# A four-layer graph network on one Trainium2 core: another quarter product by seven products, an order of sums, and an exchange of two products

## The chip, the cores and the metric

The kernel runs on one core of one Trainium2 chip. The metric is the device time of one execution in microseconds, and lower is better. TensorE does the matrix products (the profile calls it PE, and its weight loads PEld), VectorE (DVE) the additions and subtractions, ScalarE (ACT) copies out of PSUM, GpSimd (POOL) and SyncE (SP) mainly issue transfers between memory and the chip.

## The reference

Four layers follow one another, on `x` of 8 batches, 2048 nodes and 64 features and on one adjacency matrix `adj` of 2048 x 2048, in fp32. Cut to the first layer, and to the products by `adj` of the others:

```python
# layer 0: weights by node, from an embedding; Chebyshev terms x, A x, 2 A (A x) - x
for _ in range(2, K):                       # K = 3
    As.append(2.0 * (A @ As[-1]) - As[-2])
x_g = jnp.einsum('knm,bmc->bnkc', A_stack, x)
out = jnp.einsum('bnki,nkio->bno', x_g, w) + b
x = _layernorm(x + out, axis=-1)
# layer 1: twice  h = A z;  z = relu(h W_i)           then layernorm(x + z)
# layer 2: x W_self + (A x) W_neighbor + bias         then layernorm(x + ...)
# layer 3: x, A x, 2 A (A x) - x, each twice, by W    then layernorm(x + ...)
```

With the 8 x 64 = 512 columns of `x` side by side, every layer needs one or two products of the 2048 x 2048 matrix by a 2048 x 512 one, seven in all. What concerns this change is the first of them, `A x` of layer 0, and the place where the second, `A (A x)`, begins.

## The kernel before

All products by `adj` are done after Strassen: the matrix is cut into quarters A11, A12, A21, A22, the right side `x` into four quarters too, and seven products of sums of quarters take the place of eight. The sums of adj's quarters are S1 = A21 + A22, S2 = S1 - A11, S4 = A12 - S2 and S3 = A11 - A21. Inside a quarter product the same is done once more with blocks of 512 x 512; the sums of a quarter's blocks are made by `inner` (four VectorE additions, the tile `si` in the profile), those of the quarters by `outer` (the tile `so`).

The first product is different from the later ones, since the sums of `adj` don't exist yet. It runs over four slices of `adj` (`ns` = 0 to 3); each slice has 128 rows out of every 512 and comes in four chunks `ch[0]` to `ch[3]` of 1 MB, by column blocks of 512. While TensorE multiplies a slice, VectorE makes the sums of the slice (`prepare`), and POOL writes them to memory (`comb`), from which the later products fetch them. `prepare` is a generator; `put(q, s)` writes the sums of quarters and makes and writes their inner sums. Its steps are called between the products with `next(parts)`. Every addition in it is held in the program's order on VectorE.

Slice 0 is `plain_slice`: two column chunks by plain matmuls, 512 columns wide, then four quarter products by seven products (`two_level`). The chunk's first two tile rows and the rows of `x` that go with them come in small transfers, so that TensorE can begin early: chunk (0,2) on SP's queue in parts of 1, 1 and 2 tile rows (L162), and `x` on ACT's queue as the first 128 columns of tile row 0, the rest of it, tile row 1, and tile rows 2 and 3 (L167). Before the data is there TensorE runs a few matmuls on zeros (`rise`).

Slices 1 to 3 are `fast_slice`, with six products (bank `ps_n`, 16 matmuls of 256 columns each) and one by seven products (bank `ps_i`, 28 matmuls of 128 columns), in this order: p2 = A12 by x(1,0); q3 = A22 by t4, by seven products; pa = A11 by x(0,0), copied to `p1`; pc = S1 by t1; pb = S2 by t2; pe = S4 by x(1,1); and S3 by t3, onto the bank of pb. `done(blk, ...)` adds a product in PSUM to a sum and writes one quarter of the result `hT`. The sums t1 to t4 of x's quarters lie in `T`; `t1` (a different name in the code) are sums of x's blocks, which slice 0 uses and which lie in the second slot of `xy`.

What is left over between the products is done by the `pump`: it holds generators, and `pump.step()` after each half product takes one step of them. `back(ns, p, hT)` is such a job: four transposes of `hT` into `pt_n` and a copy by ScalarE into the second slot of `xy`, where the right side of the next product is put together. Slice 2's four are held back until after slice 3's q3. `keep_t1` stores `hT` to memory. After slice 3 its pairs 0 and 1 go back through `pump.drain()`, its pairs 2 and 3 by `last_back` behind the next product's first step (`pt_y`). `join_bias(h, c)` adds a bias to a quarter of `x` in place, when no product reads that quarter any more.

The next product (`product`, bank names `mma`, `mmb`, `mmc`) starts with A11 by the upper left quarter of that slot.

Buffers that matter: four for the inner sums (tag `C`), three for S1 to S4 (tag `T`), five of tag `t` for `hT` (and, from slice 0 to 1, one for the weights `w3`), four banks for `ps_n`, and two that `ps_i` and `pt_n` share.

Of the kernel before, what the change touches and what calls it, by code (L numbers as in the profile page):

```python
# [9 lines left out]
F32 = mybir.dt.float32  # L10
AF = mybir.ActivationFunctionType
ALU = mybir.AluOpType
# [4 lines left out]
P = 128  # L17
# [87 lines left out]
def kernel(  # L105
# [47 lines left out]
    def slice_chunk(ns, j, parts=(TG,)):  # L153

        a = ring.tile([P, TG, NG, P], F32, tag="a", name="a")
        m = 0
        for n in parts:
            nc.sync.dma_start(a[:, m : m + n], slices[ns, j][:, m : m + n])
            m += n
        return a  # L160
# [1 line left out]
    chunks = {}  # L162

    AHEAD = (2, 3, 0, 1)
    chunks[0, AHEAD[0]] = slice_chunk(0, AHEAD[0], (1, 1, 2))

    for t, n, cols in ((0, 1, slice(0, 2 * F)), (0, 1, slice(2 * F, BF)), (1, 1, slice(0, BF)), (2, 2, slice(0, BF))):  # L167
        t += AHEAD[0] * TG
        nc.scalar.dma_start(xy[:, 0, t : t + n, cols], x[:, t : t + n, cols])
    for j in AHEAD[1:]:  # L170
# [414 lines left out]
    if True:  # L585
# [48 lines left out]
        def prepare(ns, ch, outers):  # L634

            ch = [c.rearrange("p m i n -> p i m n") for c in ch]

            def add(out, a, b, op=ALU.add):

                tc.keep_in_program_order(nc.vector.tensor_tensor(out, a, b, op))  # L640

            def kept(tag, shape, bufs):
                s = sums.tile([P, *shape, GW], F32, tag=tag, name="s" + ("i" if tag == "C" else "o"), bufs=bufs)
                n = "ab"[: len(shape)]
                return s, s.rearrange(f"p {' '.join(n)} (m n) -> p {' '.join(n)} m n", m=TG)

            def keep(q, s0, src):
                dst = comb[q][s0 : s0 + src.shape[1]].rearrange("s p (n c) -> p s n c", n=TG)
                nc.gpsimd.dma_start(dst[:, :, ns], src)

            def inner(q, q00, q01, q10, q11):
                flat, s = kept("C", (4,), 4)
                add(s[:, 0], q10, q11)
                add(s[:, 1], s[:, 0], q00, ALU.subtract)
                add(s[:, 2], q00, q10, ALU.subtract)
                add(s[:, 3], q01, s[:, 1], ALU.subtract)
                if q is not None:
                    keep(q, 4, flat)
                return flat

            def raw(I, J):
                return [ch[2 * J + b][:, 2 * I + a] for a in range(2) for b in range(2)]

            def outer(a, b, op, tag="T"):

                flat, s = kept(tag, (2, 2), 3 if tag == "T" else 4)
                for c in range(2):
                    add(s[:, :, c], a(c), b(c), op)
                return flat

            def rq(I, J):
                return lambda c: ch[2 * J + c][:, 2 * I : 2 * I + 2]

            def sq(s):
                return lambda c: s[:, :, c].rearrange("p a (m n) -> p a m n", m=TG)

            def put(q, s):
                flat = s.rearrange("p a b c -> p (a b) c")
                keep(q, 0, flat[:, :2])
                keep(q, 3, flat[:, 3:])  # L680
                inner(q, *(flat[:, k].rearrange("p (m n) -> p m n", m=TG) for k in range(4)))


            outers[A22] = inner(A22, *raw(1, 1))
            yield
            inner(A12, *raw(0, 1))
            if ns == 0:

                sums_of_blocks()
                outers[A11] = inner(A11, *raw(0, 0))  # L690
                outers[A21] = inner(None, *raw(1, 0))
            outers[S1] = s1 = outer(rq(1, 0), rq(1, 1), ALU.add)
            outers[S2] = s2 = outer(sq(s1), rq(0, 0), ALU.subtract)
            outers[S4] = s4 = outer(rq(0, 1), sq(s2), ALU.subtract)
            if ns == 0:

                s3 = outer(rq(0, 0), rq(1, 0), ALU.subtract, "C")
            yield
            put(S1, s1)
            yield  # L700
            put(S2, s2)
            if ns:
                inner(A11, *raw(0, 0))
            yield
            if ns:
                outers[S3] = s3 = outer(rq(0, 0), rq(1, 0), ALU.subtract)
                yield
            put(S3, s3)
            if ns == 0:
                yield  # L710
            put(S4, s4)
            yield

        with tc.tile_pool(name="p_n", bufs=4, space=PSUM) as p_n, tc.tile_pool(
# [62 lines left out]
            def bank():  # L777
                return p_n.tile([P, GW], F32, tag="mm", name="ps_n")
# [13 lines left out]
            def by_tiles(v):  # L792

                return v.rearrange("p (a b) c -> p a b c", b=2)
# [10 lines left out]
                [by_tiles(xy[:, 0, j * TG : (j + 1) * TG, ts(2 * c + p, 2 * F)]) for j in range(2) for p in range(2)]  # L805
                for c in range(2)
            ]
            t1 = [[by_tiles(xy[:, 1, c:NT:TG, ts(n, 2 * F)]) for n in range(4)] for c in range(2)]
            b4 = [T[3][:, 2 * j : 2 * j + 2, :, ts(p, 2 * F)] for j in range(2) for p in range(2)]
            t4 = xs.tile([P, 4, TG, 2 * F], F32, tag="t4", name="t4")  # L810
            t4 = [by_tiles(t4[:, n]) for n in range(4)]
# [84 lines left out]
            def fast_slice(ns, ch, held, rest):  # L896
# [5 lines left out]
                def raw(I, J):  # L902
                    return lambda j, m: ch[2 * J + j][:, m, 2 * I : 2 * I + 2]

                def summed(q):
                    return lambda j, m: outers[q][:, :, j, ts(m, P)]

                def x_of(h, c):
                    return lambda k, p: xcol(0, h * NT // 2 + k, 2 * c + p)

                def t_of(n):
                    return lambda k, p: T[n - 1][:, k // 2, k % 2, ts(p, 2 * F)]

                def mul(ps, a, b, start=True, steps=2):

                    for p in range(2):
                        for k in range(NT // 2):
                            nc.tensor.matmul(  # L918
                                ps[:, ts(p, GW // 2)], b(k, p), a(k // TG, k % TG),
                                start=(start and p == k == 0), stop=(k == NT // 2 - 1),  # L920
                                skip_group_check=True,
                            )
                        if p < steps:
                            pump.step()
                    return ps

                hT = {}
# [27 lines left out]
                for job in held:  # L955
                    pump.add(back(*job))
                next(parts)
                pa = mul(bank(), raw(0, 0), x_of(0, 0))
                p1 = sums.tile([P, GW], F32, tag="p1", name="p1")
                nc.scalar.copy(p1, pa)  # L960
                nc.vector.tensor_tensor(q3, q3, p1, ALU.add)
                done(0, p2, p1)
                if ns == TG - 1:
# [9 lines left out]
                pb_ = mul(bank(), summed(S2), t_of(2))  # L973
                u2 = plus("u2", pb_, p1)
                nc.vector.tensor_tensor(u2, pc, u2, ALU.add)
                nc.vector.tensor_tensor(p1, pc, p1, ALU.add)
                next(parts)
                pe = mul(bank(), summed(S4), x_of(1, 1))
                done(1, pe, u2)
                if ns == TG - 1:  # L980
                    join_bias(1, 0)
                mul(pb_, summed(S3), t_of(3), start=False)

                done(2, pb_, q3)
                done(3, pb_, p1)
                return [hT[p] for p in range(NP)]

            last_pairs = []
            for ns in range(TG):
                ch = [chunks.pop((ns, j)) for j in range(NG)]  # L990
                if ns == 0:
                    outers = {}
                    parts = prepare(ns, ch, outers)
                    for _ in range(2):
                        next(parts)
                    first4 = plain_slice(ns, ch, outers)
                    next(first4)
                    sums_of_x(0)
                    sums_of_x(1)
                    next(parts)  # L1000
                    next(first4)
                    sums_of_x(2)
                    sums_of_x(3)
                    sums_t(b4, t4)
                    next(first4)
                    next(parts)
                    hT = next(first4)
                    next(parts)
                    w3 = load_weights()
                    load_chunks(1, *AHEAD)  # L1010
                    pump.add(biases())
                else:
                    hT = fast_slice(ns, ch, held, parts if ns == 1 else ())
                for p in range(NP):
                    keep_t1(ns, p, hT[p])

                held = []
                for p in range(NP):
                    if ns == TG - 2:
                        held.append((ns, p, hT[p]))  # L1020
                    elif ns == TG - 1 and p >= NP // 2:
                        last_pairs.append(hT[p])
                    else:
                        pump.add(back(ns, p, hT[p]))
            join_bias(1, 1)
            pump.drain()

# [238 lines left out]
```

## Time and profile before

| what | us |
|---|---|
| median of 3 runs | 1666.83 |
| lowest and highest | 1666.49, 1666.88 |
| profiled execution | 1666.76 |
| its span, first to last instruction | 1665.0 |
| mean granted clock of TensorE | 0.999 |
| first matmul on data (`plain_slice`) | at 5.92 |
| second tile row's first matmul | at 9.81 |
| slice 1 begins (first matmul of p2) | at 58.96 |
| q3 of slice 1, first matmul | at 68.00 |
| pa of slice 1, first matmul | at 74.80 |
| slice 2 begins | at 111.09 |
| slice 3 begins | at 160.54 |
| first transposes of slice 3's result | at 209.99 |
| next product (`mma`), first matmul | at 211.71 |

The span is one execution under the profiler; the time of that execution is 1.76 us longer than its span, which the work before the first and after the last instruction makes up. Times in the text are from the start of the span. "us, x96" beside a line number means 96 instructions of that line; a matmul of the program appears as two records.

### The profile page before, as it was taken

The numbers are of one execution on the slowest core, as the hardware profiler recorded it, in microseconds if no ns is written. First come the engines' busy times: TensorE is split into PE (matmuls) and PEld (weight loads), VectorE is DVE, ScalarE is ACT, GpSimd is POOL, SyncE is SP. The second block draws the span as 40 slices with busy tenths as digits, with TensorE's granted clock in tenths as the row PEclk, the third lists the DMA queues.
The fourth block names the chain that finished last, engine by engine and source line by source line (L and its number), as shares of the span: only waits on it lengthen the run. The fifth ranks groups of instructions, "written<-read, shape, count | busy, mean of one in ns | idle before, by whom it ended". The sixth has DMA issues, their size and how long they took to land.

```text
span 1665.0 us, 21271 instructions
## 1 busy us (share of the span) xinstructions
PE 1656.7 (100%) x8414; PEld 1060.6 (64%) x8414; DVE 965.9 (58%) x1737; ACT 276.0 (17%) x810; POOL 246.1 (15%) x332
## 2 busy tenths in 40 slices
PE   9999999999999999999999999999999999999998
PEld 5988844444444444444454455599998455579998
DVE  5986895656456456655434365873668344453657
ACT  0200110242142144430010011220001011100001
POOL 1221200254155056550000000000000000000000
PEclk9999999999999999999999999999999999999999
DMA  8998899504503600019877867657888866678884
GB/s 318 340 383 310 316 322 326 200 26 162 205 26 129 250 26 26 26 65 364 290 266 278 304 254 257 229 218 272 291 297 299 306 209 233 230 264 294 316 311 167
DMA packets 81074, 391.56 MB, mean 235 GB/s; under 512 B 8944, under 2 KB 25584, under 8 KB 41040
## 3 DMA queue, kind: packets, MB, share of 16 engines
q1 hardware_dynamic: 68288, 346.78, 58.2%
q0 software_dynamic: 11248, 42.08, 6.7%
q10 hardware_dynamic: 1440, 1.35, 0.3%
q8 instruction: 67, 1.10, 0.3%
q14 instruction: 31, 0.25, 0.0%
HBM read 339.85 MB, written 50.33 MB: 234 GB/s over the span
## 4 chain that ended last, share of the span: by engine, by line
PE 95%; DVE 3%; DMA 1%; issue 0%; SPq 0%; DVEq 0%
PE y L1109 20%; PE mmb L277 17%; PE mma L277 12%; PE mmc L277 12%; PE mmb L270 9%; PE ps_n L918 7%; PE mma L270 6%; PE mmc L270 6%; PE z L1161 3%; PE z L1190 2%; PE ps_i L832 1%; DVE si L640 1%; DMA xy<-in_x 1%; PE pt L1152 1%; DMA bias<-in_b_l 0%; DVE so L640 0%
## 5 line engine op out<-in xcount | busy, mean ns | idle before, releaser
L277 PE MATMUL mmb<-a,t 128*128 128x512 f32 x648 | 292.0, 593 | 0.0
L1119 DVE SCALAR_TENSOR_TENSOR xy<-y,e_sb,xy 128x128 f32<-128x128 f32 x512 | 179.6, 351 | 141.2 <-PE y L1109 125.3
L277 PEld LDWEIGHTS mmb<-a,t 128*128 128x128 f32 x648 | 121.5, 190 | 145.3 <-issue 143.5
L1128 POOL TENSOR_TENSOR s<-s 128x512 f32<-128x512 f32 (+2 forms) x192 | 157.4, 820 | 333.0 <-ACT s L1123 322.8
L1123 ACT ACTIVATE s<-y,e_sb 128x128 f32<-128x128 f32 x512 | 139.3, 383 | 231.5 <-PE y L1109 231.5
L228 DVE TENSOR_TENSOR u<-mmb,p 128x512 f32<-128x512 f32 x84 | 57.9, 689 | 176.5 <-PE mmb L277 121.1
L270 PE MATMUL mmb<-t,a 128*128 128x128 f32 x1344 | 156.9, 275 | 0.0
L270 PEld LDWEIGHTS mmb<-t,a 128*128 128x128 f32 x1344 | 153.5, 192 | 0.0
L1109 PE MATMUL y<-wn,xT 64*128 64x512 f32 x512 | 131.5, 590 | 0.0
L1109 PE MATMUL y<-wn,C 64*128 64x512 f32 x512 | 131.2, 589 | 0.0
L1109 PE MATMUL y<-wn,tT 64*128 64x512 f32 x512 | 131.2, 589 | 0.0
L277 PE MATMUL mma<-a,T 128*128 128x512 f32 x256 | 115.5, 594 | 0.0
L277 PE MATMUL mmc<-a,t 128*128 128x512 f32 x216 | 97.3, 592 | 0.0
L295 ACT COPY p<-mma 128x512 f32<-128x512 f32 x42 | 24.7, 588 | 405.8 <-PE mma L277 248.4
L1109 PEld LDWEIGHTS y<-wn,xT 64*128 64x128 f32 x512 | 49.3, 187 | 61.2 <-issue 60.7
L1109 PEld LDWEIGHTS y<-wn,tT 64*128 64x128 f32 x512 | 49.6, 187 | 60.2 <-issue 60.2
L1109 PEld LDWEIGHTS y<-wn,C 64*128 64x128 f32 x512 | 49.5, 187 | 60.3 <-issue 60.3
L277 PE MATMUL mma<-a,xy 128*128 128x512 f32 x192 | 86.6, 594 | 0.3 <-PE pt_n L465 0.3
L277 PEld LDWEIGHTS mma<-a,T 128*128 128x128 f32 x256 | 47.6, 190 | 56.8 <-issue 56.5
L228 DVE TENSOR_TENSOR C<-mmc,C 128x512 f32<-128x512 f32 x48 | 33.2, 692 | 85.9 <-PE mmc L277 75.1
L277 PEld LDWEIGHTS mmc<-a,t 128*128 128x128 f32 x216 | 40.0, 190 | 45.4 <-issue 45.2
L277 PEld LDWEIGHTS mma<-a,xy 128*128 128x128 f32 x192 | 36.0, 190 | 44.4 <-issue 43.8
(160 smaller groups left out, 2127.5 us busy)
## 6 DMA issues: line engine op xcount, KB each, us to landing
a<-comb SPq DMA_DIRECT2D x240, 1024.0 KB, 4.8
a<-in_blocks SPq DMA_DIRECT2D x54, 1024.0 KB, 4.8
comb<-si POOLq DMA_DIRECT2D x28, 1024.0 KB, 6.2
a<-in_slices SPq DMA_DIRECT2D x15, 1024.0 KB, 9.0
comb<-so POOLq DMA_DIRECT2D x15, 512.0 KB, 9.6
t1T<-hT SPq DMA_DIRECT2D x16, 256.0 KB, 4.6
xT<-in_xT SPq DMA_DIRECT2D x16, 256.0 KB, 3.0
tT<-t1T SPq DMA_DIRECT2D x16, 256.0 KB, 3.1
```

What stands on the lines that cost most here:

```text
L228: nc.vector.tensor_tensor(out, a, b, op)
L270: nc.tensor.matmul(to, a[:, k, m, :], xb[:, m, :], start=(start and opens and m == 0), stop=(m == TG - 1), skip_group_check=True,)
L277: nc.tensor.matmul(ps, xb[:, m, :], a[:, :, m, :], start=(start and m == 0), stop=(m == TG - 1), skip_group_check=True,)
L295: nc.scalar.copy(p1, pa)
L640: tc.keep_in_program_order(nc.vector.tensor_tensor(out, a, b, op))
L918: nc.tensor.matmul(ps[:, ts(p, GW // 2)], b(k, p), a(k // TG, k % TG), start=(start and p == k == 0), stop=(k == NT // 2 - 1), skip_group_ ...
L1109: mm = nc.tensor.matmul(y[:, b, :], terms[n][half, ts(k, P)], wn[half, n, h * DH : (h + 1) * DH, :], start=(n == 0), stop=(n == 2),)
L1119: nc.vector.scalar_tensor_tensor(acc, y[:, :, ts(d, F)], e, acc, ALU.mult, ALU.add)
L1123: nc.scalar.activation(s[:, d], y[:, :, ts(d, F)], AF.Copy, scale=e)
L1128: nc.gpsimd.tensor_tensor(s[:, :n], s[:, :n], s[:, n : 2 * n], ALU.add)
L1161: nc.tensor.matmul(z[:, k, :], aT[:, ts(k, P)], wd[:, w, :], start=(n == 0), stop=(n == len(terms) - 1),)
L1190: nc.tensor.matmul(z[n][:, k], xT[half, ts(k, P)], w[half], start=True, stop=True)
```

## The change

Four things are changed, all within the first product and the step to the second.

1. The first chunk comes in parts of 1 and 3 tile rows instead of 1, 1 and 2, and the rows of `x` beside it as two parts of tile row 0 and one of tile rows 1 to 3.
2. In slice 1, A11's inner sums are made right after A12's, ahead of S1, and A11 by x(0,0) becomes a `two_level` product, with the block sums `t1` that slice 0 has left. For that the two halves of `t1` change places: what belongs to columns 0 now lies where slice 1's own result will be put, and not where slice 0's goes. The product has no pump steps of its own.
3. In slice 0, `put(S3)` comes before `put(S2)`; one call of `next(parts)` at its end falls away, so that `put(S2)` and `put(S4)` are both done in slice 1, after A22's inner sums.
4. In slice 3 the last two products change places: S3 by t3 comes before S4 by x(1,1) and gets a bank of its own, with `q3` plus the S2 product made by an addition of its own. The results of pairs 0 and 1 are then complete before the last product, and their store and their `back` jobs are put in there, two to a half product (`n=2`).

```diff
-    chunks[0, AHEAD[0]] = slice_chunk(0, AHEAD[0], (1, 1, 2))
+    chunks[0, AHEAD[0]] = slice_chunk(0, AHEAD[0], (1, 3))
-    for t, n, cols in ((0, 1, slice(0, 2 * F)), (0, 1, slice(2 * F, BF)), (1, 1, slice(0, BF)), (2, 2, slice(0, BF))):
+    for t, n, cols in ((0, 1, slice(0, 2 * F)), (0, 1, slice(2 * F, BF)), (1, 3, slice(0, BF))):
...
             inner(A12, *raw(0, 1))
+            if ns == 1:
+                outers[A11] = inner(A11, *raw(0, 0))
...
             put(S1, s1)
             yield
+            if ns == 0:
+                put(S3, s3)
+                yield
             put(S2, s2)
-            if ns:
+            if ns > 1:
                 inner(A11, *raw(0, 0))
             yield
             if ns:
                 outers[S3] = s3 = outer(rq(0, 0), rq(1, 0), ALU.subtract)
                 yield
-            put(S3, s3)
-            if ns == 0:
-                yield
+                put(S3, s3)
             put(S4, s4)
             yield
...
-            t1 = [[by_tiles(xy[:, 1, c:NT:TG, ts(n, 2 * F)]) for n in range(4)] for c in range(2)]
+            t1 = [[by_tiles(xy[:, 1, 1 - c : NT : TG, ts(n, 2 * F)]) for n in range(4)] for c in range(2)]
...
-                def mul(ps, a, b, start=True, steps=2):
+                def mul(ps, a, b, start=True, steps=2, n=1):
...
-                            pump.step()
+                            pump.step(n)
...
-                pa = mul(bank(), raw(0, 0), x_of(0, 0))
-                p1 = sums.tile([P, GW], F32, tag="p1", name="p1")
-                nc.scalar.copy(p1, pa)
+                p1 = new_out("p1")
+                if ns == 1:
+                    two_level(
+                        lambda i, j: lambda m: ch[j][:, m, i], outers[A11], b1[0], t1[0], by_blocks(p1)
+                    )
+                else:
+                    pa = mul(bank(), raw(0, 0), x_of(0, 0))
+                    nc.scalar.copy(p1, pa)
...
-                nc.vector.tensor_tensor(p1, pc, p1, ALU.add)
-                next(parts)
-                pe = mul(bank(), summed(S4), x_of(1, 1))
-                done(1, pe, u2)
                 if ns == TG - 1:
+
+                    nc.vector.tensor_tensor(q3, pb_, q3, ALU.add)
+                    next(parts)
+                    ps3 = mul(bank(), summed(S3), t_of(3))
+                    done(2, ps3, q3)
+                    for p in range(2):
+                        keep_t1(ns, p, hT[p])
+                        pump.add(back(ns, p, hT[p]))
+                    done(3, ps3, u2)
                     join_bias(1, 0)
-                mul(pb_, summed(S3), t_of(3), start=False)
-
-                done(2, pb_, q3)
-                done(3, pb_, p1)
+                    pe = mul(bank(), summed(S4), x_of(1, 1), n=2)
+                    done(1, pe, u2)
+                else:
+                    nc.vector.tensor_tensor(p1, pc, p1, ALU.add)
+                    next(parts)
+                    pe = mul(bank(), summed(S4), x_of(1, 1))
+                    done(1, pe, u2)
+                    mul(pb_, summed(S3), t_of(3), start=False)
+                    done(2, pb_, q3)
+                    done(3, pb_, p1)
...
                     hT = next(first4)
-                    next(parts)
                     w3 = load_weights()
...
-                for p in range(NP):
+                for p in range(0 if ns < TG - 1 else 2, NP):
                     keep_t1(ns, p, hT[p])
```

More of the change, by code (lines that the diff above doesn't have):

```diff
@@ L1020 @@
                         held.append((ns, p, hT[p]))
-                    elif ns == TG - 1 and p >= NP // 2:
+                    elif ns < TG - 1:
+                        pump.add(back(ns, p, hT[p]))
+                    elif p >= 2:
                         last_pairs.append(hT[p])
-                    else:
-                        pump.add(back(ns, p, hT[p]))
             join_bias(1, 1)
```

## The prediction

> **What bounds the kernel now.** I read the page first: the shares of the engines and of the chain of waits. One row of each says that TensorE is the bound and that almost nothing else is on the path.
>
> ```profile
> PE 1656.7 (100%) x8414; PEld 1060.6 (64%) x8414; DVE 965.9 (58%) x1737; ACT 276.0 (17%) x810; POOL 246.1 (15%) x332
> ...
> PE 95%; DVE 3%; DMA 1%; issue 0%; SPq 0%; DVEq 0%
> ```
>
> TensorE is idle for 1665.0 - 1656.7 = 8.3 us in all. The view of waits, TensorE alone, names only three of them over the whole span:
>
> ```profile
> PE rise L724 <- DVE zero L721: 1.1, 1, 1.1
> PE ps_i L832 <- DVE si L640: 0.3, 1, 0.3
> PE mma L277 <- PE pt_n L465: 0.3, 1, 0.3
> ```
>
> So a change can gain only by giving TensorE less work, by closing the second and third wait, or by a better start. All edits lie in the first 216 us; what follows shifts as a block. The chain in order of time gives the price of TensorE's work there and shows the hand-over from the last slice to the next product (start, duration, what):
>
> ```profile
> 118.60 6.25 PE ps_i L832 x56
> ...
> 189.43 20.74 PE ps_n L918 x96
> 210.17 0.02 issue
> 210.19 0.43 DVE hT L934
> ...
> 210.67 0.78 PE pt_n L465 x4
> ...
> 211.71 3.67 PE mma L277 x8
> 215.38 0.87 PE pt_y L1051 x8
> ```
>
> A quarter product by seven products (28 matmuls of 128 columns, two records each) is the x56: 6.25 us. A plain quarter product (16 matmuls of 256 columns, two records each) is a third of the x96: 6.91 us. At 210.17 the last product ends; VectorE's hT and four transposes stand between it and mma. In the timeline of slice 1 I read where VectorE feeds TensorE and how late it is (start, duration, instruction):
>
> ```profile
> 68.53 0.69 DVE L640 TENSOR_TENSOR si<-si,a 128x512 f32<-128x512 f32 x1
> ...
> 69.37 1.13 PE L832 MATMUL ps_i<-si,t 128*128 128x128 f32 x8 [0.31 <-DVE si L640]
> ...
> 82.58 3.62 PE L918 MATMUL ps_n<-so,T 128*128 128x256 f32 x16
> ```
>
> The second sum of A22 starts at 68.53 and the product that needs it at 69.37, 0.84 us later. VectorE has no idle time from 28.10 to past 100 us: around slice 1 it is a second, close bound. Last, the DMA view of the first 16 us (KB each, us from issue to landing), and the two hardware queues between 9 and 10 us (packets, MB), q1 being SP's and q10 ACT's:
>
> ```profile
> xy<-in_x ACTq DMA_DIRECT2D x1, 512.0 KB, 10.2
> xy<-in_x ACTq DMA_DIRECT2D x1, 256.0 KB, 8.0
> xy<-in_x ACTq DMA_DIRECT2D x1, 192.0 KB, 4.8
> ```
>
> ```profile
> q1 hardware_dynamic: 34, 0.28, 65.7%
> q10 hardware_dynamic: 35, 0.14, 33.8%
> ```
>
> The two queues move equal numbers of packets: a queue with larger packets gets more of the bytes.
>
> **What the Trainium skill says.** "DMA: Bandwidth & Descriptors", section "Queues, rings and completion order": each DMA engine goes round-robin over the queues that have work, packet by packet. The 34 against 35 packets agree. "TensorE: Matmul & The Clock Gate", Part 1: TensorE falls to half its clock after an idle window of about 3.4 us. The trace agrees that the first 22 matmuls run at half speed (22 in 4.7 us, 0.21 us apart, against 6.25/56 = 0.112 us later); that a gap in mid-kernel costs anything, no row of it shows. "VectorE: DVE Perf Modes", the section on the SBUF errata, gives (N+151)/0.96 ns for an fp32 tensor_tensor, 691 ns at 512; the trace has 0.69, one begun every 0.605 us.
>
> **The change part by part**, against the profiled execution, 1666.76 us (span 1665.0 and 1.76 around it; the median shown is 1666.83).
>
> *Start.* Chunk (0,2) comes in two transfers instead of three, and the x rows in three instead of four: tile rows 1 to 3 together. Now, the 256 KB of row 1 are issued at about 1.66 and land 8.0 us later, at 9.7, and the row's first matmul starts at 9.81; rows 2 and 3, issued at about 2.16, land at 12.4. After the change the second tile row waits for all three. Counting bytes in turn, packet against packet: m0 with x row 0's first part (0.33 MB); then m1-3 in 6 KB packets against 1.5 KB ones of the rest of row 0 (0.98 MB); then 8 KB packets of the next x block against 6 KB ones of rows 1 to 3 (1.84 MB): 3.15 MB, as many as when rows 2 and 3 land now. Larger packets move at 420 to 450 GB/s rather than 300 to 344 (windows of 1 us), worth 0.5 us at most, so landing is 11.9 to 12.4 and the second tile row starts at about 12.1. TensorE is then 12.1 - 9.8 = 2.3 us late; bounds 1.5 (the rows land as soon as their bytes are through, at 11.3) and 3.3. The rest of row 0 lands later too (about 7.5 to 8.5 for 6.0), but that gap lies inside the 2.3 us. In slice 0 nothing cuts this down: after 9.81 TensorE never waits there. SP's next loads go out sooner, but its queue is busy throughout; for VectorE, which waits for x until 23.66, I take 0.2 us earlier (0 to 0.5).
>
> *Slice 1, VectorE.* put(S3) takes the place of put(S2) in slice 0, and put(S2) moves into slice 1, behind A22's sums. Up to the end of A12's sums it is the same set of instructions, so that point stays at 75.41; A22's sums come 4 x 0.605 = 2.4 us sooner, which ends the 0.31 us wait. Its worth: that product took 74.80 - 68.00 = 6.80 us from its start to the next, against 6.25: 0.55 us. A11's four sums now begin at 75.41, the second at 76.13, and with the 0.84 us above the product by S-sums can start at 76.97. They need a C buffer: with four of them, the one of A22, whose write to memory (issued 68.19, 5.9 us) lands by 74.1 and whose product ends by then or, shifted, near 76.5. S1, S2 and S4 come 2.4 us later (S1 by 79.8); TensorE wants S1 after 82. No cost.
>
> *Slice 1, TensorE.* The plain product of A11 (6.91) gives way to seven products (6.25): -0.65. Two transposes' steps move into later products, cost nothing, but done(0) now waits for them, about 1.4 us; put(S2)'s place is empty, so S3 is still ready near 96 and wanted at 105. Without any wait the second of the seven would start at 68.00 + 6.25 + 0.89 = 75.14, plus the late start, 2.3: 77.4, after VectorE's 76.8. So TensorE sets it: slice 1 ends 2.3 - 0.55 - 0.65 = 1.1 us later than now. Were the start not late at all, the wait for A11's sums would come instead: 76.97 - 76.34 = 0.63 us later than now (76.34 is where that start would have to be to break even, 75.14 + 0.55 + 0.65). Start and wait hide each other, they don't add.
>
> *Last slice.* S3's product comes before S4's, in a bank of its own; q3 takes S2's product by one more addition (0.69), p1's is dropped: VectorE even. The transposes of pairs 0 and 1 go into the middle of S4's product. VectorE before them: two additions, q3's and the two puts, 6.9 us beside S3's 6.9: just hidden. At the end mma follows the product at once. Now pt_n starts at 209.99 and mma at 211.71; eight transposes are 0.87, so 0.85 is saved, and with mma's own slow first step 0.9. The next sums of xy are wanted 3.43 + 0.87 = 4.3 us after; behind done(1) 0.75 and join_bias 2.28 they would end at 5.0, a wait of 0.7, unless VectorE takes them in its pause during S4's product. I take 0, since the trace has such independent work run ahead already: four of pt_n's transposes, two of each pair, ran before the wait at 210.19, which is not the program's order.
>
> Sum: +1.1 - 0.9 = +0.2 us, 1667.0 us.
>
> **The rivals.** (1) *VectorE sets slice 1.* If the rows land by about 11.3 instead of 12.0, TensorE meets A11's wait: +0.6 - 0.9, 1666.5; and if TensorE puts ready transposes or raw products into the wait, or VectorE gets its x sooner, down to +0.0 - 0.9, or 1665.6. For it: VectorE's unbroken row. Against: 9.7 and 12.4 are landings that I read, and the bytes are the same. (2) *Slower: the start runs cold.* The new gaps (about 1 us near 7, 1.7 near 10.4) bring the half clock back; a window of 3.4 us at half speed costs 1.7. With a start that is 3.3 late this is 1.0 + 1.7 more: 1669.7; with 2.3, 1668.7. It decides from gaps that fill a window; at 1.7 us they are half of one. (3) *The hand-over doesn't close*, because VectorE's sums wait behind join_bias: 0.7 back, 1667.7. (4) *Clearly faster.* All gains and no cost: -0.65 - 0.55 - 0.9 - 0.35 (the gap at 9.5) = -2.5, 1664.3; still under 0.2%. Nothing in the profile holds more.
>
> **How the numbers follow.** My forecast 0.5, (1) 0.25, (2) 0.1, (3) 0.1, the rest 0.05. Range 1665.4 to 1668.8. About 0.2%, 3.3 us, is what a measurement of this kernel can tell from no change. (4) doesn't reach it and only (2) at its worst does; for instructions ordered in ways that I don't see I leave 0.06 for faster and 0.1 for slower.
>
> **What would show it.** TensorE's second tile row at 12 us rather than 9.8; the ps_i product of A22 with no wait on si; the next, on A11, with none or less than 0.5 us; 56 records where 32 were; pt_n in the middle of the S4 product and mma 0.0 to 0.1 us after its end. I am wrong if the second tile row starts before 11, if A11's sums hold TensorE by over 1 us, or if the matmuls of 512 columns between 7 and 15 us come 0.86 us apart instead of 0.43.

## The result and the profile after

The changed kernel takes 1671.82 us (median of 7 runs, 1670.18 to 1674.39); the kernel before, run beside it, 1666.83 (1666.27 to 1667.0). The ratio is 1.0030, with a 95% interval of 1.0019 to 1.0041: slower by 5.0 us, where 0.2 us was predicted. The profiled execution took 1670.74 us, 3.98 more than the one of before (span 1668.9 for 1665.0), so the trace holds four of the five microseconds. The rest lies in how the executions spread, and the experiments come back to it.

The page of the kernel after, busy time and shares of the chain of waits:

```profile
PE 1655.3 (99%) x8438; PEld 1059.6 (63%) x8438; DVE 966.4 (58%) x1739; ACT 277.5 (17%) x816; POOL 245.6 (15%) x332
...
PE 95%; issue 2%; DMA 2%; DVE 1%; POOL 0%; ACTq 0%; DVEq 0%; POOLq 0%
```

TensorE has 1.4 us less busy time than before (the A11 product was to bring 0.65 of it), but 5.3 us more of idle time: 13.6 instead of 8.3. The view of waits, TensorE alone (us in total, times, longest), says where:

```profile
PE ps_n L875 <- DMA xy<-in_x: 3.7, 2, 2.2
PE ps_i L835 <- DVE si L640: 1.1, 1, 1.1
PE rise L727 <- DVE zero L724: 1.1, 1, 1.1
PE mma L277 <- PE ps_n L921: 0.9, 1, 0.9
PE ps_i L835 <- ACT part L839: 0.4, 1, 0.4
```

Two waits for `x` at the start are new. The wait for `si` of before (0.3, for A22's sums) is gone, and one for A11's sums stands in its place. The wait of mma, 0.3 behind the transposes, has become 0.9 behind the product. The timeline of the start (start, duration, instruction, idle time before it), with the transfers of the same stretch (KB, us from issue to landing):

```profile
5.12 1.12 PE L875 MATMUL ps_n<-a,xy 128*128 128x512 f32 x2
7.68 2.84 PE L875 MATMUL ps_n<-a,xy 128*128 128x512 f32 x6 [1.43 <-DMA xy<-in_x]
12.76 3.67 PE L875 MATMUL ps_n<-a,xy 128*128 128x512 f32 x8 [2.24 <-DMA xy<-in_x]
```

```profile
xy<-in_x ACTq DMA_DIRECT2D x1, 768.0 KB, 10.9
...
xy<-in_x ACTq DMA_DIRECT2D x1, 192.0 KB, 6.4
```

The second tile row starts at 12.76 instead of 9.81: 2.95 us. The 192 KB that ran beside it took 6.4 us instead of 4.8. Slice 1 begins at 61.88 (58.96 before), so 2.92 of it arrive there. In slice 1, the timelines of TensorE and VectorE, and the chain of waits for that stretch:

```profile
77.17 1.06 PE L835 MATMUL ps_i<-a,xy 128*128 128x128 f32 x8
78.58 0.49 PE L835 MATMUL ps_i<-a,xy 128*128 128x128 f32 x2 [0.35 <-ACT part L839]
80.14 1.16 PE L835 MATMUL ps_i<-si,xy 128*128 128x128 f32 x8 [1.07 <-DVE si L640]
...
85.37 3.62 PE L921 MATMUL ps_n<-so,T 128*128 128x256 f32 x16
```

```profile
76.17 0.69 DVE L640 TENSOR_TENSOR si<-a,si 128x512 f32<-128x512 f32 x1
78.67 0.69 DVE L640 TENSOR_TENSOR si<-a 128x512 f32<-128x512 f32 x1 [1.81 <-DMA comb<-si]
79.39 0.69 DVE L640 TENSOR_TENSOR si<-si,a 128x512 f32<-128x512 f32 x1
```

```profile
72.08 6.56 DMA comb<-si
...
78.67 0.70 DVE si L640
```

The last of A12's sums is begun at 76.17 and the first of A11's not before 78.67: it waits for a write to memory, issued at 72.08, whose source is the buffer that it needs. That is the write of S2's inner sums, which VectorE had made from 69.17 to 71.8; the write of A22's was issued at 69.55. A product by seven products takes 6.25 us; this one takes 85.37 - 77.17 = 8.20. So 1.95 us are lost here, more than the two products gain (0.55 and 0.65). At the end of the last slice, the chain and the timeline:

```profile
211.24 3.47 PE ps_n L921 x16
214.71 0.88 issue
215.59 3.67 PE mma L277 x8
```

```profile
214.74 0.75 DVE L937 TENSOR_TENSOR hT<-ps_n,u 128x256 f32<-128x256 f32 x2 [0.16 <-PE ps_n L921]
...
215.59 3.67 PE L277 MATMUL mma<-a,xy 128*128 128x512 f32 x8 [0.89 <-PE ps_n L921]
```

No transpose stands between the product and mma, and mma still starts 0.88 after the product's end, when VectorE is through with `done(1)` (214.74 + 0.75 = 215.49). From the start of slice 2 to mma it is 100.83 us, against 100.62 before: the exchange costs 0.2 instead of bringing 0.9.

The sum of the trace: 2.92 - 0.55 - 0.65 + 1.95 + 0.21 = 3.88, for 3.9 between the spans.

### The profile page after: what moved, and what is told of

It is laid out like the page before. It is cut to its first block, busy times and chain, and to the rows that moved or that the text cites. A ratio compares the mean times of both kernels' runs of the same rounds, so it can differ in the third digit from the quotient of the medians.

```text
span 1668.9 us, 21330 instructions
## 1 busy us (share of the span) xinstructions
PE 1655.3 (99%) x8438; PEld 1059.6 (63%) x8438; DVE 966.4 (58%) x1739; ACT 277.5 (17%) x816; POOL 245.6 (15%) x332
## 4 chain that ended last, share of the span: by engine, by line
PE 95%; issue 2%; DMA 2%; DVE 1%; POOL 0%; ACTq 0%; DVEq 0%; POOLq 0%
PE y L1127 20%; PE mmb L277 17%; PE mma L277 12%; PE mmc L277 12%; PE mmb L270 9%; PE ps_n L921 7%; PE mma L270 6%; PE mmc L270 6%; PE z L1179 3%; PE z L1208 2%; PE ps_i L835 1%; PE pt L1170 1%; DMA bias<-in_b_l 1%; DMA xy<-in_x 1%; DVE si L640 1%
```

## The experiments

The theory after the two traces: three terms of the sum were wrong, each in its own place (start, A11's buffer, hand-over). The rivals were that the late start brings about the other two, by shifting TensorE against VectorE, and that the spread of the times comes from the start. Every kernel computes the whole result. `fill_gap` does more than is needed: nine matmuls whose result nobody reads. The kernels were measured in three groups, each on a chip of its own with the kernel before beside it: `start_only`, `start_undone`, `seven_only` and `exchange_only` (before: 1666.57 us, 54 runs), `c_in_T`, `fill_gap`, `exchange_pc` and `best2` (1666.55, 54 runs), and `before_own`, `exchange_own` and `best3` (1666.48, 41 runs). Ratios and differences are against the kernel before of the same group.

### The parts alone

`start_only`: the kernel before with the new transfers of the start (both lines of part 1).

> The kernel before with the start of the kernel after alone (transfers of 1 and 3 tile rows). If the late second tile row is worth what the trace of after shows (12.76 for 9.81, 2.95 us) and only the 0.55 us wait of slice 1 is hidden by it: 2.4 us above before, 1669.2 us, with the A22 product of slice 1 no longer waiting. If the new gaps also let TensorE's clock fall in some executions, the times spread by 2 us or more and the median lies above 1669.5. If later slack took the late start in: under 1667.5.

Measured: 1669.09 us (1668.69 to 1670.86, 16 runs), ratio 1.0018 [1.0011, 1.0026]. +2.5 for the start alone, and the wait for A22's sums is gone with it: q3 runs without a wait from 70.59 to 76.85. A late TensorE meets a VectorE that is ready. Ten executions lie between 1668.69 and 1669.36 with a mean clock of 0.999 or more, six between 1670.42 and 1670.86 with 0.998; the profiled one is of the ten.

`start_undone`: the kernel after with the old start.

```diff
-    chunks[0, AHEAD[0]] = slice_chunk(0, AHEAD[0], (1, 3))
+    chunks[0, AHEAD[0]] = slice_chunk(0, AHEAD[0], (1, 1, 2))
-    for t, n, cols in ((0, 1, slice(0, 2 * F)), (0, 1, slice(2 * F, BF)), (1, 3, slice(0, BF))):
+    for t, n, cols in ((0, 1, slice(0, 2 * F)), (0, 1, slice(2 * F, BF)), (1, 1, slice(0, BF)), (2, 2, slice(0, BF))):
```

> The kernel after with the start of the kernel before. Theory: the sums of A11 wait for a C buffer that the sums of S2 are still being written from; they would do so without the late start too, since put(S2) is then only 1.4 us earlier (buffer free near 77.3, the product of A11 goes on at 78.9 against 76.3 to break even), so only 1.2 of the 3.9 us go: about 1669.5, and the times lie within 1 us. Rival, the late start is the whole cost and adds: 1667.8. Rival, the start also brings VectorE's work forward so far that the buffer is free in time: under 1667.

Measured: 1670.2 us (1668.33 to 1671.67, 15 runs), 1.0019 [1.0011, 1.0027]. By the medians, undoing the start gives back only 1.4 us of the 5.0 (3.6 over the kernel before remain). Between executions of like mean clock it is about 2: 1668.48 (median of five) against 1670.74 (of three) at 0.999, and 1670.40 (of ten) against 1672.48 (of four) below. The rest of the start's 2.9 is lost again, because TensorE now comes earlier to the same wait. That the times would lie within 1 us did not come true. The timeline of TensorE in slice 1, and its granted clock in stretches of 2 us (behind the stretch its length and the busy times of PE, PEld, DVE, ACT and POOL, each with its count; then the clock as a fraction of full speed, the DMA share and GB/s):

```profile
74.36 1.06 PE L835 MATMUL ps_i<-a,xy 128*128 128x128 f32 x8
75.77 0.49 PE L835 MATMUL ps_i<-a,xy 128*128 128x128 f32 x2 [0.35 <-ACT part L839]
78.12 1.35 PE L835 MATMUL ps_i<-si,xy 128*128 128x128 f32 x8 [1.86 <-DVE si L640]
...
84.99 3.62 PE L921 MATMUL ps_n<-so,T 128*128 128x256 f32 x16
```

```profile
76.00:78.00 2.00, 0.26 (x2) 0.07 (x1) 1.32 (x3) 0.00 (x0) 0.32 (x1) 1.00 1.02 385
78.00:80.00 2.00, 1.88 (x12) 1.88 (x13) 2.00 (x4) 0.27 (x1) 0.43 (x1) 0.74 0.99 371
80.00:82.00 2.00, 2.00 (x11) 2.00 (x11) 2.00 (x3) 0.27 (x1) 0.48 (x2) 0.50 0.95 350
82.00:84.00 2.00, 2.00 (x19) 2.00 (x18) 2.00 (x3) 0.53 (x2) 1.11 (x2) 0.91 1.00 369
```

A11's product takes 10.63 us here, 4.38 more than the unhindered 6.25. The pause is 2.7 of that (75.25 to 78.12, less the two records of one matmul in it); after it the clock is granted at half speed. From the three clocks, half speed lasted (0.26 + 0.50 + 0.09) x 2 / 0.5 = 3.4 us and cost 1.7.

`seven_only`: the kernel before with the second product by seven products and the new order of the sums (parts 2 and 3, which were not run one without the other).

> The kernel before with A11 by seven products in slice 1 and the new order of the sums alone (start and last slice as before). Theory: the A11 sums wait for their C buffer until about 77.3 us, TensorE for them about 3.7 us, less 0.55 and 0.65: 2.5 us above before, 1669.3. Rival, VectorE's place alone decides (sums at 75.4, no buffer wait): 1667.4.

Measured: 1669.76 us (1668.08 to 1671.28, 20 runs), 1.0017 [1.0010, 1.0023]. The same pause, in another execution:

```profile
76.25 0.49 PE L835 MATMUL ps_i<-a,xy 128*128 128x128 f32 x2 [0.35 <-ACT part L839]
78.54 1.16 PE L835 MATMUL ps_i<-si,xy 128*128 128x128 f32 x8 [1.80 <-DVE si L640]
...
83.78 3.62 PE L921 MATMUL ps_n<-so,T 128*128 128x256 f32 x16
```

```profile
80.00:82.00 2.00, 2.00 (x21) 2.00 (x20) 2.00 (x3) 0.53 (x2) 0.74 (x1) 1.00 0.97 356
```

This time the clock stayed at 1.00. The 20 times form two groups: nine from 1668.08 to 1668.78, the profiled one (1668.78, with a wait of 0.8 us for `x` at its start) among them, and eleven from 1669.72 to 1671.28. The distance of the groups, 1.8 us between their medians, is about the 1.7 of one stretch at half speed, and the mean clock over the span tells them apart without an exception: 0.999 in all nine, 0.998 in all eleven (0.001 of the span is 1.7 us). In `start_undone` it is the same, five times at 0.999 up to 1668.66 and ten at 0.998 or 0.997 from 1669.63, the profiled one among these. On this chip the kernels with this pause had the lower clock in 21 of 35 executions, while `exchange_only` and the kernel before, which have neither the pause nor the new start, had it in none of 66.

`exchange_only`: the kernel before with part 4.

> The kernel before with the exchange of the last two products of slice 3 alone. Theory: the next product's first bank is the one S4's product was in, and waits for VectorE to read it (two additions, 0.75 us): mma follows the last product after about 0.9 us, nothing is saved, 1666.8 to 1667.1. Rival, the forecast's hand-over: mma follows at once, 1665.9.

Measured: 1666.74 us (1666.48 to 1667.29, 12 runs), 1.0002 [0.9993, 1.0010]. Not the 0.9 that the prediction counted on.

The parts alone, by their medians +2.5, +3.2 and +0.2, make 5.9; together they are +5.0. The traces account for 0.2 of this difference. A11's product takes 8.94 us in `seven_only` (83.78 - 74.84) and 8.20 behind the late start, so 0.74 of the start is hidden in the wait; but the 0.55 of A22's product is gained in each of the first two kernels, and together only once. The other 0.7 is put down here to the share of executions at the lower clock, which moves a median; no run shows that by itself. The start doesn't bring about the other losses, since each of them is there without it, and the spread isn't the start's alone.

### Which buffer A11's sums wait for

In the compiled program, where every tile has its address, A11's sums have the address of S2's inner sums, and not of A22's. The trace of after agrees: the write that they wait for is the one of 72.08. A22's buffer is still to be read by q3's product, which comes later in the program; S2's inner sums are read by the write alone. `c_in_T` gives A11's sums of slice 1 a buffer of the tag `T`, which is free.

```diff
-            def inner(q, q00, q01, q10, q11):
-                flat, s = kept("C", (4,), 4)
+            def inner(q, q00, q01, q10, q11, tag="C"):
+                flat, s = kept(tag, (4,), 4 if tag == "C" else 3)
...
-                outers[A11] = inner(A11, *raw(0, 0))
+                outers[A11] = inner(A11, *raw(0, 0), tag="T")
```

> The kernel after with A11's sums of slice 1 in a buffer of tag T, so that they need no C buffer; VectorE's order is the same. Theory: the 1.8 us wait of VectorE for the write of S2's sums goes; TensorE's second of the seven products starts 1.56 us after the sums begin, near 78.3, instead of at 80.1: the fastest runs 1.8 us under those of after (1670.2), 1668.4, and since hardly a pause is left (0.3 us), the clock stays up: median within 0.5 us of the fastest, all under 1669.5. Rival, VectorE's place in the order holds TensorE, not the buffer: over 1670. Rival, the spread comes from the start: it stays at 3 us or more.

Measured: 1668.79 us (1668.52 to 1670.71, 20 runs), 1.0014 [1.0007, 1.0021]. VectorE and TensorE in slice 1:

```profile
76.04 0.68 DVE L640 TENSOR_TENSOR si<-a,si 128x512 f32<-128x512 f32 x1
76.64 0.69 DVE L640 TENSOR_TENSOR so<-a 128x512 f32<-128x512 f32 x1
```

```profile
77.03 1.06 PE L835 MATMUL ps_i<-a,xy 128*128 128x128 f32 x8
78.20 1.13 PE L835 MATMUL ps_i<-so,xy 128*128 128x128 f32 x8
...
83.63 3.62 PE L921 MATMUL ps_n<-so,T 128*128 128x256 f32 x16
```

A11's sums (`so` now, by their buffer's name) follow A12's without a gap, and the product takes 6.60 us instead of 8.20. VectorE later waits 3.62 us for a buffer of tag `T` instead (at 87.42), which holds up no product. The median over the kernel before falls from 5.0 to 2.2, more than the 1.6 that the trace gains. 18 of the 20 times lie within 0.9 us; the other two, 1670.39 and 1670.71, are above the 1669.5 that was expected as the limit and have a mean clock of 0.998. The buffer was the cause of the wait, and with the wait most of the executions at the lower clock are gone: 2 of 20, against four of seven of the kernel after, whose runs were not made beside these.

`fill_gap` leaves the wait and puts matmuls into it, on the base of `start_undone`:

```diff
                 mul(pa, 0, b11, True, part[:, 0])
+                for r in range(9 if fill is not None else 0):
+                    tc.keep_in_program_order(
+                        nc.tensor.matmul(fill[:, :P], ident, ident, start=True, stop=True)
+                    )
                 mul(pb_, 5, t2, True, part[:, 1])
```

> The kernel after with the start of before (start_undone, 1670.2 us, 1668.3 to 1671.7), with nine matmuls of the unit matrix, 2.0 us, put into TensorE's pause of slice 1; their result isn't used. If the pause of about 2.9 us lets the clock fall in some executions (half speed from 79 to 82.5 us in that kernel's trace, 1.7 us lost) the fill keeps it up: 1668.3 to 1668.8, spread under 1 us, though TensorE has more to do. If the spread comes from the landing times of the writes: unchanged, about 1670.2 with 3 us of spread.

Measured: 1668.93 us (1668.53 to 1672.6, 17 runs), 1.0016 [1.0009, 1.0023]. Fifteen times lie between 1668.53 and 1669.31, where `start_undone` had five of fifteen below 1669. The profiled execution is one of the other two (1672.41):

```profile
75.45 2.17 PE L844 MATMUL ps_n<-ident 128*128 128x128 f32 x18
80.11 1.13 PE L835 MATMUL ps_i<-si,xy 128*128 128x128 f32 x8 [2.49 <-DVE si L640]
```

VectorE was some 2.1 us later in this execution (the write of S2's sums was issued at 72.63, instead of 70.50), so that 2.49 us of wait were left after the fill, and the clock fell all the same (0.83, 0.50, 0.82 from 80 to 86 us). The mean clock is 0.999 or 1.0 in the fifteen and 0.998 in the two. A pause that is mostly filled goes with a fall of the clock in 2 executions of 17, an open one in 10 of 15. The two kernels ran on different chips, so this comparison alone could be the chips'; but on the first chip, too, the falls came with the pause (21 of 35 against none of 66). So the pause is what raises their number. It isn't the only thing that brings them on: on the second chip one of 54 executions of the kernel before has a mean clock of 0.998 (1670.51).

### What mma waits for

The exchange put `S4`'s product into the bank that mma takes over. If that is the wait, another bank ends it; `exchange_pc` is `exchange_only` with one line changed:

```diff
-                    pe = mul(bank(), summed(S4), x_of(1, 1), n=2)
+                    pe = mul(pc, summed(S4), x_of(1, 1), n=2)
```

> The kernel before with the exchange alone, S4's product in the bank of the S1 product instead of in one of its own, so that the next product's first bank was left long before. Theory: mma follows S4's product at once, 0.9 us less than with the exchange alone (1666.74): 1665.85. Rival, the wait at mma has another cause (the transposed tiles, a load): still 1666.7.

Measured: 1666.76 us (1666.46 to 1667.29, 12 runs), 0.9999 [0.9991, 1.0008]. The theory fell:

```profile
211.65 3.67 PE L277 MATMUL mma<-a,xy 128*128 128x512 f32 x8 [0.90 <-PE ps_n L918]
```

In the compiled program of this kernel mma's bank (0) had its last user long before, and the instruction ahead of mma still waits for VectorE to have ended `done(1)`. The pool `p_mm` is opened where `p_n` was closed, and what its first tile waits for is the last reader of the closed pool, whichever bank that read. So the test is a bank for mma that never belonged to the closed pool:

```diff
+        p_m1 = ctx.enter_context(tc.tile_pool(name="p_m1", bufs=1, space=PSUM))
+        n_banks = [0]
-        with tc.tile_pool(name="p_n", bufs=4, space=PSUM) as p_n, tc.tile_pool(
+        with tc.tile_pool(name="p_n", bufs=3, space=PSUM) as p_n, tc.tile_pool(
...
-                return p_n.tile([P, GW], F32, tag="mm", name="ps_n")
+                n_banks[0] += 1
+                return (p_n if n_banks[0] % 4 != 1 else p_m1).tile([P, GW], F32, tag="mm", name="ps_n")
...
-        p_mm = ctx.enter_context(tc.tile_pool(name="p_mm", bufs=2, space=PSUM))
+        p_mm = ctx.enter_context(tc.tile_pool(name="p_mm", bufs=1, space=PSUM))
...
-                pool = p_mm if p_mm2 is None or banks % 3 else p_mm2
+                pool = p_mm2
+                if p_mm2 is None or banks % 3:
+                    mmt += 1
+                    pool = p_m1 if mmt % 2 else p_mm
```

The rotation of the banks is as before; only the pools are cut otherwise. `exchange_own` is `exchange_only` with it.

> Before, with the exchange of the last slice alone and the bank of its own for mma. Theory (after the exchange mma waits for done(1) because its bank belongs to the pool that closes, whatever bank the product had): the wait of mma of 0.9 us on ps_n is gone or under 0.1, mma starts within 0.1 of the end of the product, and the time is 0.9 lower than before, 1665.65. Rival (the 0.9 us are mma's own start, a weight load or a transfer): the wait stays at 0.9 and the time at 1666.7.

Measured: 1665.70 us (1665.41 to 1670.69, 13 runs), 0.9996 [0.9988, 1.0004]. The interval of the ratio reaches over 1, so the time alone does not tell this from no change; the trace does. No wait of mma is left; it follows the product, and `done(1)` runs beside it:

```profile
208.76 2.10 PE L924 MATMUL ps_n<-so,xy 128*128 128x256 f32 x9
210.70 3.60 PE L277 MATMUL mma<-a,xy 128*128 128x512 f32 x8
```

```profile
210.91 0.76 DVE L940 TENSOR_TENSOR hT<-ps_n,u 128x256 f32<-128x256 f32 x2 [0.17 <-PE ps_n L924]
```

`before_own` is the kernel before, without any part of the change, with the same bank.

> Before, with the next product's first bank taken out of the pool that closes: one bank of its own (p_m1) for mma and for every fourth ps_n, three instead of four in p_n. Theory (mma waits for the last VectorE read of the closed pool, done(3), whose end at 211.63 is 0.08 before mma's start at 211.71): mma starts when the last transposes end, near 211.45, so -0.25 us, 1666.3. Rival (mma waits for nothing of the pool): no change, 1666.55. If three rotating banks are too few, a wait on DVE or ACT appears at ps_n in slices 1 to 3 and the time is over 1666.8.

Measured: 1665.62 us (1665.25 to 1666.64, 13 runs), 0.9994 [0.9985, 1.0002]: -0.86, three times what was expected, though this interval, too, reaches just over 1. TensorE at the end of the last slice:

```profile
209.52 0.60 PE L468 MATMUL pt_n<-ident,hT 128*128 128x128 f32 x4
209.95 1.02 PE L277 MATMUL mma<-a,xy 128*128 128x512 f32 x2
210.81 0.60 PE L468 MATMUL pt_n<-ident,hT 128*128 128x128 f32 x4
211.25 2.74 PE L277 MATMUL mma<-a,xy 128*128 128x512 f32 x6
```

TensorE fills the time in which it waits for `hT` with the first matmul of mma (two records), which I had not counted. So the gap at the hand-over could be had without the exchange: the bank is worth 0.86 with the order of before and, between the two groups, 0.95 with that of the change (from +0.17 to -0.78). No gain of the order shows. Two of the thirteen executions of `exchange_own`, 1669.10 and 1670.69, have a mean clock of 0.998; no trace of such an execution was kept, and what brought them on is open.

### A version that beats both

`best2` is the kernel after with the old start, A12's sums of slice 1 moved behind those of A11, S1, S2 and S4, and S4's product in the bank of S1's:

```diff
-            inner(A12, *raw(0, 1))
+            if ns != 1:
+                inner(A12, *raw(0, 1))
             if ns == 1:
                 outers[A11] = inner(A11, *raw(0, 0))
...
                 s3 = outer(rq(0, 0), rq(1, 0), ALU.subtract, "C")
+            if ns == 1:
+                inner(A12, *raw(0, 1))
```

> The change with three mends: the start of before, A12's sums in slice 1 behind those of A11 and S1, S2, S4 (so that A11's come 2.4 us earlier and find a C buffer free), and S4's product of the last slice in the bank of the S1 product. Theory: no wait of TensorE in slice 1, 0.55 + 0.65 + 0.9 less than before: 1664.6, spread under 1 us. Rival, another buffer or sum is late next (A12's sums late, chunks of slice 2 later): 1665.5 or more.

Measured: 1665.69 us (1665.26 to 1666.86, 13 runs), 0.9995 [0.9987, 1.0004]. Slice 1 takes 109.62 - 58.70 = 50.92 us, against 52.13 before: the 1.2 of the two products, in full. The 0.9 of the hand-over was missing here, and the interval reaches over 1. `best3` has the bank of its own instead of S1's.

> The changed kernel with the old start, A12's sums of slice 1 behind A11's, S1's, S2's and S4's, and the bank of its own for mma. Theory: no wait in slice 1 (-1.2) and none at mma (-0.9): 1664.5 us, 2.1 below before. Rival (the hand-over keeps its 0.9): 1665.7. If three rotating banks bring a wait: over 1665.7.

Measured: 1664.37 us (1664.01 to 1666.01, 21 runs), 0.9987 [0.9980, 0.9993]: 2.1 us below the kernel before, the only one of these with an interval wholly below 1, and, by the two comparisons, some 7 below the changed one. It keeps the exchange; whether it would be as fast without it was not tried. All that the view of waits lists for TensorE, and its A11 product in slice 1:

```profile
PE rise L735 <- DVE zero L732: 1.1, 1, 1.1
```

```profile
73.79 1.06 PE L844 MATMUL ps_i<-a,xy 128*128 128x128 f32 x8
74.68 1.06 PE L844 MATMUL ps_i<-si,xy 128*128 128x128 f32 x8
...
80.04 3.62 PE L930 MATMUL ps_n<-so,T 128*128 128x256 f32 x16
```

## Why the prediction was wrong, step by step

The forecast was 1667.0, the profiled execution took 1670.74. Of these 3.7 us, 1.95 are the wait for A11's buffer, 1.1 the hand-over, and 0.65 the size of the start; the median's further 1.1 goes with the lower clock.

1. *The start, 2.3 us with bounds of 1.5 and 3.3.* The mechanism held, the size was short, though within its bounds: 2.95 in the profile of after, 2.63 in that of `start_only` (12.44 for 9.81), whose 2.5 over the kernel before has the gain at A22's product in it. The landing was taken from the bytes alone; the second tile row of after started 0.66 later than the 12.1 of the prediction. The gain for VectorE held: x's last sums begin at 23.38 rather than 23.66.
2. *"They need a C buffer: with four of them, the one of A22 [...] No cost."* This is the step that failed. I took the oldest buffer by counting, and put the wait for it at nothing; the program gave out another, since the oldest was still to be read by A22's product. S2's was taken, 2.5 us younger, and its write (issued 72.08, 6.56 us) ended too late. Cost: 1.95 us in the profiled execution, and, by the mean clocks, in others a stretch at half clock on top. The prediction named the sign of it ("if A11's sums hold TensorE by over 1 us") and not the cause.
3. *VectorE's point of 75.41.* It was said to stay; A12's sums ended 1.36 later, at 76.77, since in slice 0 VectorE must wait for the late TensorE (1.67 us for ScalarE's copy in `two_level`). Behind the late start A11's sums would have held TensorE by 0.35 even with a free buffer (`c_in_T`).
4. *"Start and wait hide each other, they don't add."* Half right. They overlap, by 0.74 of the 2.9 us, and not wholly, because the wait ends with the write, at 78.6 with the new start and at about 76.6 with the old one: VectorE moves with TensorE.
5. *The two products, -0.55 and -0.65.* Both held; slice 1 of `best2` is 1.21 shorter than before, without a wait.
6. *The hand-over, -0.9, "At the end mma follows the product at once".* Failed: +0.2. That the next sums of xy run ahead held (211.95, before the product's end), as did the transposes in the middle of the product. What I didn't see is that mma waits for the last read of the closed pool. The trace before had it, in VectorE's timeline:

```profile
210.87 0.75 DVE L934 TENSOR_TENSOR hT<-ps_n,p 128x256 f32<-128x256 f32 x2
```

   This is `done(3)`; it ends at 211.62, and mma starts at 211.71. I put mma's wait down to the transposes, which the view of waits names.
7. *Rivals.* That a pause brings the half clock back, at 1.7 us, was named, at the start alone and at a chance of 0.1. It is shown in slice 1, where the pause comes from the buffer. At the start no trace shows it: the six higher times of `start_only`, 1.6 above the others and at the lower clock, have no other new pause than those of the start, but none of them was profiled. The rival of join_bias did not occur. The lower end of rival (1) was summed wrongly: +0.0 - 0.9 from 1666.76 is 1665.9, not 1665.6; nothing hangs on it. That the first 22 records run at half speed was read from their distance alone; the granted clock of the same trace is given as 1.00 there, and no run here settles which of the two is right. The range ended at 1668.8 because it held only one late wait at a time.

The 1.1 us between the profiled execution of the kernel after and its median fit such stretches: three of its seven runs lie at 1670.18 to 1670.92 with a mean clock of 0.999, three at 1671.82 to 1672.5 with 0.998, and one at 1674.39 with 0.997. Whether it was the pause at the start or the one in slice 1 that each of them had stays open.

## What to carry to other kernels

When sums are moved forward, look up which buffer they get in the new order, in the compiled program or in the trace: here it was not the oldest, which a product still had to read, but one with a write under way. Then ask when that transfer ends. Before reordering work to close a gap at a hand-over between stages, look for what ended just ahead of the first instruction on every engine: here it was the last read of a pool that closes, and a bank outside of that pool brought the gain with no reordering. A pause on the bounding engine is to be priced with what may follow it, not by its length alone.

## What was not expected of the hardware

TensorE's clock fell to 0.50 for some 3.4 us after a pause of 2.9 us in which it still ran one matmul, two records (75.25 to 78.12 in `start_undone`, by the records' 0.112 us), and did not fall after the same pause of 2.8 us in the profiled execution of `seven_only`. The Trainium skill, "TensorE: Matmul & The Clock Gate", Part 1, speaks of an idle window of about 3.4 us; the length at half clock agrees with that, but the pause that brought it on was shorter. The page also has the window run freely, which fits that one pause hits in some executions alone; where a window begins no run here shows. And a 1 MB write of inner sums took 5.9 us in the kernel before (A22's) and 6.56 after (S2's): an interval of that size in a sum needs bounds of its own.
